# Where thirteen blocks of a cleared matrix are issued from, and when, in a graph network with expert layers on one core

## Chip, core and metric

The kernel runs on one NeuronCore of a Trainium2 chip. The metric is the device time of one execution in microseconds. TensorE (PE in the profile, its weight loads PEld), VectorE (DVE), ScalarE (ACT) and GpSimd (POOL) each have an instruction queue of their own; SyncE (SP) only issues DMAs here. DMAs issued by GpSimd are indirect ones (gathers and scatters by an index per partition).

## The reference

6250 nodes with 256 features, 100000 edges `(src, dst, edge_weight)` sorted by `dst`. The first of four layers is a graph layer, and the change lies in it. Cut to what matters:

```python
def _L0_gnn_ref(x, edge_row, edge_col, edge_vals, eps, W1, b1, g1, be1, W2, b2, g2, be2):
    msgs = edge_vals[:, None] * x[edge_col]
    agg = jax.ops.segment_sum(msgs, edge_row, num_segments=n)
    h = (1.0 + eps[0]) * x + agg
    h = _bn_relu(h @ W1 + b1, g1, be1)
    h = _bn_relu(h @ W2 + b2, g2, be2)
    return h
# called as  x = x + _L0_gnn_ref(_layernorm(x), src, dst, edge_weight, ...):
# edge_row is src, edge_col is dst
```

So every node collects, over its edges, the weighted feature rows of its neighbours. A layer of 8 experts (2 per token), a second pair of graph convolutions and a layer of 4 experts follow; the change leaves them as they are.

## The kernel before

**Two ways to sum.** The edges stand in 782 groups of 128. `dst` is sorted and dense at low numbers, so the first 395 groups (`C0`) fall on only 13 blocks (`DB`) of 128 neighbours. For those, the kernel builds a matrix `S` in DRAM: 13 blocks of 128 x 6272 cells, one cell for each pair of neighbour and node, and a spare row of cells at its end. The weights are scattered into `S`, and TensorE multiplies blocks of `S` with the neighbours' rows (`product_of_cells`). For the other groups, `scatter_items` makes 423 items, each a product and a scatter of 128 rows of 256 floats that are added into three accumulators in DRAM (`acc`, L716).

**Clearing S.** `clear_cells(b, z)` (L564) writes zeros over block `b`: one DMA of 3136 KB from a small zero tile `zz`. Block 0 and the spare tail (L834) are cleared at the start; the blocks 1 to 12 are cleared in `later_loads` (L843) after the loads of `X`. All of it is issued by SyncE. The dictionary `zeros` keeps the DMA of each block, so that scatters can wait for it.

**Comparing keys.** `cell_values(c0, c1, ...)` (L522) handles a chunk of four groups (`CB`). SyncE loads the chunk's cell keys, broadcast to all partitions (`h_kb`, L530); VectorE compares them with the keys of each edge (`h_eq`, L538, four per chunk); TensorE sums the weights of edges with the same key (`h_pa`, L544); ScalarE copies the result out (`h_sa`, L546); TensorE turns it (`h_pt`, L549); VectorE writes the values `hv` (L550, L552) and the places `hc` (L555). From group 72 (`CA`) on, a group is also compared with the group ahead of it.

**Scattering.** `scatter_cells(c)` (L572) lets GpSimd scatter the 128 values of group `c` into `S`. Groups under 72 add (`OP.add`), as groups close to each other may share cells: they are taken in four lanes of 18 groups, and each waits for the landing of the one ahead of it in its lane. The later groups only write (`OP.bypass`) and wait for nothing but the clearing of the blocks that they can reach: block `b` from group `LO[b]` on, which is 105, 152, 187, 217, 244, 267, 289, 310, 329, 347, 364 and 381 for the blocks 1 to 12.

**The order of the work.** First all chunks under group 72 are compared, then `later_loads` is called, then come the adding scatters (with seven gathers of the later items between them, L423), then the layer norm of the nodes. After that `rows_to_cells(72, 395)` (L873) goes through the other chunks: it compares up to 16 groups ahead (`AHEAD`) and scatters behind. From about group 142 on, each scatter also advances `product_of_cells` by 0.8 steps. A step loads parts of a block from `S` (`sb`, L632; on SyncE, after all scatters emitted so far), turns them (`ctp`, L641), copies them out on ScalarE (`st`, L643), multiplies (`cps`, L615) and adds to `X` on VectorE (L620). The three accumulators are cleared on the way (L184). The instructions are ordered by a scheduler, which may move an instruction ahead of others on its engine unless `tc.keep_in_program_order` pins it; waits follow from the order in which the program emits what touches the same memory.

Of the kernel before, what the change touches and what calls it, by code (L numbers as in the profile page):

```python
# [14 lines left out]
P = 128  # L15
# [28 lines left out]
DB = 13  # L44
C0 = 395
CA = 72
CB = 4
RATE0 = 0.8
RATE1 = 0.85
AHEAD = 4  # L50

SETS = [(0,), (1, 2), (3, 4, 5), (6, 7, 8), (9, 10), (11, 12)]
LANES = 4
# [2 lines left out]
SROW = NT * P  # L56
# [3 lines left out]
LO = [0] + [int(r) - 6 for r in ROW_AT[1:DB]]  # L60
# [26 lines left out]
def rows_of(t):  # L87
    return min(P, N - t * P)
# [3 lines left out]
def gnn_ffn_kernel(ctx: ExitStack, tc: tile.TileContext, a: dict, out: bass.AP):  # L92
    nc = tc.nc
# [10 lines left out]
    S = nc.dram_tensor("S", (SALL + (C0 + 1) * P,), F32, kind="Internal").ap()  # L104
# [6 lines left out]
    X = big.tile([P, NT, D], F32, name="X")  # L111
# [9 lines left out]
    def load_groups(g, src):  # L121
        t0, t1 = g * TG, (g + 1) * TG
        full = [t for t in range(t0, t1) if rows_of(t) == P]
        nc.sync.dma_start(X[:, t0:t0 + len(full), :],
                          src[t0 * P:(t0 + len(full)) * P].rearrange("(t p) d -> p t d", p=P))
        for t in range(t0 + len(full), t1):
            nc.sync.dma_start(X[:rows_of(t), t, :], src[t * P:t * P + rows_of(t)])

    def store_group(table, src, g):
        t0, t1 = g * TG, (g + 1) * TG  # L130
# [38 lines left out]
    full = const.tile([P, P], F32, name="full")  # L169
# [13 lines left out]
    def clear(k, src):  # L183
        nc.sync.dma_start(accs[k].rearrange("(p t) d -> p t d", p=P),  # L184
                          src[:, None, :].to_broadcast([P, NROW // P, D]))
# [332 lines left out]
    def across(table, r0, r1):  # L518

        return bass.AP(tensor=table.tensor, offset=table.offset + r0 * P, ap=[[0, P], [1, (r1 - r0) * P]])  # L520

    def cell_values(c0, c1, ep, ap, tp):  # L522

        n = c1 - c0
        pair = c0 >= CA
        r0 = c0 - 1 if pair else c0
        kb = ep.tile([P, CB + 1, P], F32, name="h_kb", bufs=4)
        nc.sync.dma_start(kb[:, :c1 - r0, :].rearrange("p c q -> p (c q)"), across(keys, r0, c1))  # L530
        eq = ep.tile([P, CB, 2 * P], F32, name="h_eq")
        ct = ep.tile([P, CB], F32, name="h_ct")
        wd = ep.tile([P, CB, CB], F32, name="h_wd")
        half = slice(0 if pair else P, 2 * P)
        nc.vector.tensor_tensor(wd[:, :n, :n], hw[:, c0:c1, None].to_broadcast([P, n, n]), unit[:, :n, :n], OP.mult)
        for i in range(n):
            c = c0 + i
            nc.vector.scalar_tensor_tensor(eq[:, i, half],  # L538
                                           kb[:, i:i + 1 + pair, :].rearrange("p c q -> p (c q)"),
                                           hk[:, c:c + 1], upto2[:, half], op0=OP.is_equal, op1=OP.mult,  # L540
                                           accum_out=ct[:, i:i + 1])
        pa = ap.tile([CB, 2 * P], F32, name="h_pa")
        for i in range(n):
            nc.tensor.matmul(pa[:n, half], wd[:, i, :n], eq[:, i, half], start=(i == 0), stop=(i == n - 1))  # L544
        sa = ep.tile([CB, 2 * P], F32, name="h_sa")
        nc.scalar.copy(sa[:n, half], pa[:n, half])  # L546
        pt = tp.tile([P, 2, CB], F32, name="h_pt")
        for h in range(0 if pair else 1, 2):
            nc.tensor.transpose(pt[:, h, :n], sa[:n, h * P:(h + 1) * P], ident[:n, :n])  # L549
        nc.vector.tensor_copy(hv[:, c0:c1], pt[:, 1, :n])  # L550
        if pair:
            nc.vector.tensor_tensor(hv[:, c0 - 1:c1 - 1], hv[:, c0 - 1:c1 - 1], pt[:, 0, :n], OP.add)  # L552
        nc.vector.tensor_scalar(ct[:, :n], ct[:, :n], nofit, 1.5, op0=OP.add, op1=OP.is_gt)
        nc.vector.tensor_tensor(ct[:, :n], ct[:, :n], aside[:, c0:c1], OP.mult)
        nc.vector.tensor_tensor(hc[:, c0:c1], ct[:, :n], hk[:, c0:c1], OP.add)  # L555

    zeros = {}
# [6 lines left out]
    def clear_cells(b, z):  # L564

        zw = z.shape[1]
        ins = nc.sync.dma_start(S[b * P * SROW:(b + 1) * P * SROW].rearrange("(p q w) -> p q w", p=P, w=zw),
                                z[:, None, :].to_broadcast([P, SROW // zw, zw]))
        tc.add_to_no_dep_group("cells", ins.ins)
        zeros[b] = ins.ins  # L570

# [259 lines left out]
    zz = only0.tile([P, ZW], F32, name="zz")  # L831
    nc.vector.memset(zz, 0.0)
    clear_cells(0, zz)
    rest = nc.sync.dma_start(S[SALL:].rearrange("(p q) -> p q", p=P), zz[:, :C0 + 1])  # L834
    tc.add_to_no_dep_group("cells", rest.ins)
    zeros[DB] = rest.ins
    cell_keys()
# [5 lines left out]
    def later_loads():  # L843
        nc.vector.memset(hi_i, FAR)
        g0 = EC // P
        nc.sync.dma_start(hi_i[:, :g0], ed[:g0 * P, 2 * P - 1:2 * P].rearrange("(g p) o -> p (g o)", p=P))
        nc.sync.dma_start(hi_i[:EC - g0 * P, g0:g0 + 1], ed[g0 * P:EC, 2 * P - 1:2 * P])
        for g in range(NG):
            load_groups(g, a["x"])
        nc.sync.dma_start(vec, a["vecs"])  # L850
        for b in range(1, DB):
            clear_cells(b, zz)

    with tc.tile_pool(name="cl", bufs=5) as lp, tc.tile_pool(name="clt", bufs=2, space=PSUM) as tp, \
            tc.tile_pool(name="clp", bufs=2, space=PSUM) as pp:
        product = product_of_cells(nodes, lp, tp, pp)
        next(product)
        steps = [0.0, 0]

        def advance(n, blocks=0):  # L860

            steps[0] += n
            while steps[0] >= 1:
                steps[0] -= 1
                try:
                    product.send(blocks)
                except StopIteration:
                    return

        with tc.tile_pool(name="sc", bufs=2) as ep, tc.tile_pool(name="ev", bufs=1) as gp, \  # L870
                tc.tile_pool(name="sca", bufs=2, space=PSUM) as ap, tc.tile_pool(name="sct", bufs=1, space=PSUM) as ctp:

            def rows_to_cells(c0, c1):  # L873
                cleared, valued = 0, set()
                for c in range(c0, c1, CB):
                    if c == 160:
                        item_columns(gp, ctp, evs)
                    if c >= 200 + 24 * cleared and cleared < NACC:
                        tc.keep_in_program_order(nc.vector.memset(zero, 0.0))
                        clear(cleared, zero)  # L880
                        cleared += 1
                    for e in range(c, min(c1, c + (AHEAD + 1) * CB), CB):
                        if e not in valued:
                            valued.add(e)
                            cell_values(e, min(e + CB, c1), ep, ap, ctp)
                    e = min(c + CB, c1)
                    for i in range(c - 1, e - 1 if e < C0 else e):
                        scatter_cells(i)
                        done = sum(HI[b] + 24 <= i for b in range(DB))
                        if done:  # L890
                            advance(RATE0, done)

            for j in range(0, CA // CB):
                cell_values(j * CB, (j + 1) * CB, ep, ap, ctp)
            later_loads()
            items_of_rows(ctp)
            evs = []
            for i, c in enumerate(l * LC + j for j in range(LC) for l in range(LANES)):
                if c < CA - 1:
                    scatter_cells(c)  # L900
                if i == 20:
                    evs = fetch_items(gp)
            for g in range(NG):
                mv, rstd = ln_stats(x_tiles(g))
                for i, x in enumerate(x_tiles(g)):
                    r, t = x.shape[0], g * TG + i
                    ln_apply(nodes[:r, t, :], x, mv, rstd, i)
                    nc.scalar.activation(X[:, t, :], nodes[:, t, :], AF.Copy, scale=geps)
            rows_to_cells(CA, C0)
        with tc.tile_pool(name="sg", bufs=2) as ep, tc.tile_pool(name="sw", bufs=4) as wp, \  # L910
                tc.tile_pool(name="spt", bufs=1, space=PSUM) as ptp, \
                tc.tile_pool(name="spm", bufs=2, space=PSUM) as pmp:

            def along(k):
                advance(RATE1, sum(HI[b] + 24 <= C0 + k - KF for b in range(DB)))

            scatter_items(KF, NK, nodes, (ep, wp, ptp, pmp), along)
        for _ in product:
            pass
# [42 lines left out]
    with tc.tile_pool(name="f0c", bufs=1) as fc:  # L962
# [7 lines left out]
        with tc.tile_pool(name="f0x", bufs=2) as xp, tc.tile_pool(name="f0s", bufs=1) as sp, \  # L970
# [132 lines left out]
            for e in range(X0):  # L1103
                c0 = 0
                for name, k in (("L0_ffn_ln_g", KD), ("L0_ffn_ln_b", KD), ("L0_ffn_b1", H0 // P)):
                    c = VAT[name] + e * k
# [415 lines left out]
```

## Time and profile before

| | us |
|---|---|
| median of 3 runs | 4661.52 |
| lowest, highest | 4650.03, 4668.09 |
| the profiled execution | 4696.92 |
| its span, first to last instruction | 4695.1 |
| GpSimd's first scatter into `S` (L574) | 40.26 |
| GpSimd's first scatter that only writes | 229.82 |
| last landing of the accumulators (`acc`, L716) | 1571.06 |

The table of engines at the head of the page gives busy time, share of the span and number of instructions:

```
PE 3700.9 (79%) x16130; PEld 2742.6 (58%) x16130; DVE 1950.9 (42%) x7650; ACT 1055.4 (22%) x2437; POOL 2211.6 (47%) x1914
```

The groups of instructions have one line each: line of the code, engine, operation, what is written and read, count, busy time, mean duration in ns, and the idle time of the engine just before them with what ended it. The two groups of GpSimd's queue in the first 1560 us are:

```
L716 POOL DMA_INDIRECT acc<-m,idx x423 | 657.3, 1554 | 190.0 <-issue 69.2
L574 POOL DMA_INDIRECT S<-hv,hc x395 | 429.2, 1087 | 259.4 <-issue 92.4
```

A timeline has start, duration, engine, line and operation, and in brackets the idle time ahead and its releaser. SPq is SyncE's queue of DMAs. Idle time put down to "issue" is time in which an engine waited for nothing that the profile shows.

### The profile page before, as it was taken

How to read it: one execution, taken by the hardware profiler on the slowest of the kernel's cores; microseconds unless marked ns; L12 is line 12 of the kernel's file. 1: busy time of each engine (PE TensorE's matmuls, PEld its weight loads, DVE VectorE, ACT ScalarE, POOL GpSimd, SP SyncE). 2: the span in 40 equal slices, each digit the busy share in tenths (PEclk: the TensorE clock that was granted, in tenths of full speed). 3: DMA queues.
4: the chain of work that ended last, by engine and by line, in shares of the span. 5: the costliest groups of instructions: out<-in, count | busy, mean ns of one | idle time of the engine just before them, and what ended most of it. 6: DMA issues, size and time to landing. Idle time of an engine off the chain costs nothing.

```text
span 4695.1 us, 52949 instructions
## 1 busy us (share of the span) xinstructions
PE 3700.9 (79%) x16130; PEld 2742.6 (58%) x16130; DVE 1950.9 (42%) x7650; ACT 1055.4 (22%) x2437; POOL 2211.6 (47%) x1914
## 2 busy tenths in 40 slices
PE   3407778777778576899999978888877888787999
PEld 1103446666666236788888856666646666663444
DVE  6405444334334577322121254444454444445443
ACT  2001113333333242222222230000032000005443
POOL 3676666877778200233333306666623666650000
PEclk7658889999899775999999988999998999998999
DMA  9804525666666731566667645555415554540000
GB/s 305 255 21 154 186 91 95 104 102 101 102 107 74 195 111 57 173 187 191 198 188 199 179 137 191 159 157 155 133 29 176 157 160 152 157 141 13 18 18 19
DMA packets 411033, 627.76 MB, mean 134 GB/s; under 512 B 59719, under 2 KB 317530, under 8 KB 410730
## 3 DMA queue, kind: packets, MB, share of 16 engines
q1 hardware_dynamic: 266554, 426.28, 28.1%
q0 software_dynamic: 144176, 197.85, 22.1%
q8 instruction: 140, 2.29, 0.2%
q14 instruction: 163, 1.34, 0.1%
HBM read 459.47 MB, written 165.69 MB: 133 GB/s over the span
## 4 chain that ended last, share of the span: by engine, by line
PE 53%; DVE 5%; issue 4%; DMA 3%; ACT 1%; another core or an unknown queue 0%; POOL 0%; SPq 0%; DVEq 0%; POOLq 0%; ACTq 0%
PE dps L1298 12%; PE pm L736 9%; PE ph L1199 8%; PE py L1208 8%; PE dense L270 3%; PE hid L1254 2%; PE ph L1449 2%; PE py L1474 1%; DMA g<-table,s_i 1%; PE ph L1443 1%; DVE bn_st L237 1%; PE py L1472 1%; PE pl L1006 1%; PE tp L230 1%; DMA s<-acc 1%
## 5 line engine op out<-in xcount | busy, mean ns | idle before, releaser
L731 POOL DMA_INDIRECT g<-table,s_i x846 | 804.8, 951 | 601.6 <-PE dps L1298 178.6
L716 POOL DMA_INDIRECT acc<-m,idx x423 | 657.3, 1554 | 190.0 <-issue 69.2
L1298 PE MATMUL dps<-X,wide_b 128*128 128x256 f32 (+1 forms) x2548 | 714.4, 393 | 19.3 <-issue 19.0
L736 PE MATMUL pm<-g,sw 128*128 128x256 f32 x1692 | 530.8, 404 | 224.3 <-issue 123.1
L738 DVE TENSOR_TENSOR wide<-wide,pm 128x256 f32 x846 | 354.1, 419 | 625.1 <-PE dps L1298 385.7
L1298 PEld LDWEIGHTS dps<-X,wide_b 128*128 128x128 f32 (+1 forms) x2548 | 506.0, 199 | 101.1 <-issue 26.1
L574 POOL DMA_INDIRECT S<-hv,hc x395 | 429.2, 1087 | 259.4 <-issue 92.4
L736 PEld LDWEIGHTS pm<-g,sw 128*128 128x128 f32 x1692 | 312.5, 195 | 350.9 <-issue 216.2
L602 DVE TENSOR_SCALAR sw<-lane,dl,w_e 128x128 f32<-128x128 f32 x1269 | 445.2, 364 | 115.2 <-PE dps L1298 60.4
L1199 PE MATMUL ph<-xe,we 128*128 128x256 f32 x1792 | 398.9, 381 | 0.0
L1208 PE MATMUL py<-we,hT 128*128 128x256 f32 x1792 | 396.0, 379 | 0.0
L1213 POOL DMA_INDIRECT mixed<-yo,to_i x112 | 178.1, 1590 | 450.2 <-DVE yo L1211 193.8
L615 PE MATMUL cps<-wide,st 128*128 128x256 f32 x1274 | 360.3, 410 | 19.0 <-DVE X L620 18.3
L1199 PEld LDWEIGHTS ph<-xe,we 128*128 128x128 f32 x1792 | 342.2, 191 | 47.6 <-issue 0.5
L1208 PEld LDWEIGHTS py<-we,hT 128*128 128x128 f32 x1792 | 336.2, 190 | 43.4
L752 ACT COPY hT<-tp 128x512 f32<-128x512 f32 (+1 forms) x75 | 40.6, 578 | 1362.1 <-PE tp L751 1361.9
L1201 ACT ACTIVATE hT<-ph,par 128x256 f32<-128x256 f32 x448 | 213.2, 476 | 570.8 <-PE ph L1199 565.0
L697 PE MATMUL pcs<-eq,sw 128*128 128x128 f32 x846 | 183.5, 300 | 140.8 <-DVE sw L602 96.7
L615 PEld LDWEIGHTS cps<-wide,st 128*128 128x128 f32 x1274 | 251.2, 204 | 70.1 <-DVE X L620 20.0
L712 PE MATMUL pm<-wide,cT 128*128 x846 | 268.3, 404 | 28.3 <-issue 23.8
L544 PE MATMUL h_pa<-h_eq,h_wd 128*4 128x256 f32 (+1 forms) x790 | 204.5, 398 | 108.3 <-DVE h_eq L538 103.8
L697 PEld LDWEIGHTS pcs<-eq,sw 128*128 128x128 f32 x846 | 148.1, 202 | 186.6 <-issue 97.6
(342 smaller groups left out, 4602.3 us busy)
## 6 DMA issues: line engine op xcount, KB each, us to landing
we<-in_L_ffn_W_dram SPq DMA_DIRECT2D x112, 1024.0 KB
wide_b<-S SPq DMA_DIRECT2D x182, 448.0 KB
S<-zz SPq DMA_DIRECT2D x13, 3136.0 KB
sb<-S SPq DMA_DIRECT2D x91, 448.0 KB
h_kb<-keys SPq DMA_DIRECT2D x80, 320.0 KB
acc<-zero SPq DMA_DIRECT2D x3, 6400.0 KB
s<-acc SPq DMA_DIRECT2D x72, 256.0 KB
g<-table,s_i POOLq DMA_INDIRECT x846
```

Of the source, the lines that this page charges most:

```text
L574: sc = nc.gpsimd.indirect_dma_start(out=S.rearrange("(e o) -> e o", o=1), in_=hv[:, c:c + 1], in_offset=None, compute_op=OP.add if c < CA ...
L602: nc.vector.tensor_scalar(sw, lane, dl[:, k:k + 1], w_e[:, k:k + 1], op0=OP.is_equal, op1=OP.mult)
L615: nc.tensor.matmul(ps[:, j, :], st[:, i + j, :], nodes[:, b, :], start=(y == 0), stop=(y == len(sts) - 1))
L697: nc.tensor.matmul(pc, sw, eq[:, i, :], start=True, stop=True)
L712: nc.tensor.matmul(pm, cT, nodes[:, bass.ds(bv, 1), :].rearrange("p o d -> p (o d)"), start=True, stop=True)
L716: nc.gpsimd.indirect_dma_start(out=accs[k % NACC], out_offset=bass.IndirectOffsetOnAxis(ap=idx[:, i:i + 1], axis=0), in_=m, in_offset=None ...
L731: nc.gpsimd.indirect_dma_start(out=g, out_offset=None, in_=table, in_offset=bass.IndirectOffsetOnAxis(ap=s_i[:, k:k + 1], axis=0))
L736: nc.tensor.matmul(pm[:, 0, :], sw, g, start=True, stop=True)
L738: nc.vector.tensor_tensor(at, at, pm, OP.add)
L1199: nc.tensor.matmul(ps, we1[:, k, m * P:(m + 1) * P], xe[:, k, :], start=(k == 0), stop=(k == KD - 1))
L1208: nc.tensor.matmul(ps, hT[:, m, q * P:(q + 1) * P], we2[:, m, :], start=(m == 0), stop=(m == MH - 1))
L1298: nc.tensor.matmul(ps, sb[:r, t, :], X[:r, t, :], start=(t == 0), stop=(t == NT - 1))
```

## The change

`clear_cells` issues from ScalarE's queue instead of SyncE's and is pinned in program order; so is the clear of the tail. The loop over blocks 1 to 12 goes out of `later_loads`. Instead, `clear_ahead(c)` is called ahead of the comparison of each chunk, and clears the next blocks whose first scatter `LO[b]` is at most 48 groups ahead. Block 1 so comes at group 60, blocks 2 to 12 at groups 104, 140, 172, 196, 220, 244, 264, 284, 300, 316 and 336. `load_groups` returns its DMAs; nothing uses them.

```diff
+CLEARED = 48
+
...
     def clear_cells(b, z):
 
         zw = z.shape[1]
-        ins = nc.sync.dma_start(S[b * P * SROW:(b + 1) * P * SROW].rearrange("(p q w) -> p q w", p=P, w=zw),
+        ins = nc.scalar.dma_start(S[b * P * SROW:(b + 1) * P * SROW].rearrange("(p q w) -> p q w", p=P, w=zw),
                                 z[:, None, :].to_broadcast([P, SROW // zw, zw]))
+        tc.keep_in_program_order(ins)
         tc.add_to_no_dep_group("cells", ins.ins)
         zeros[b] = ins.ins
...
     rest = nc.sync.dma_start(S[SALL:].rearrange("(p q) -> p q", p=P), zz[:, :C0 + 1])
+    tc.keep_in_program_order(rest)
     tc.add_to_no_dep_group("cells", rest.ins)
...
         nc.sync.dma_start(vec, a["vecs"])
-        for b in range(1, DB):
-            clear_cells(b, zz)
...
                     for e in range(c, min(c1, c + (AHEAD + 1) * CB), CB):
                         if e not in valued:
+                            clear_ahead(e)
                             valued.add(e)
                             cell_values(e, min(e + CB, c1), ep, ap, ctp)
...
+            def clear_ahead(c):
+
+                while len(zeros) <= DB and LO[len(zeros) - 1] <= c + CLEARED:
+                    clear_cells(len(zeros) - 1, zz)
+
             for j in range(0, CA // CB):
+                clear_ahead(j * CB)
                 cell_values(j * CB, (j + 1) * CB, ep, ap, ctp)
```

More of the change, by code (lines that the diff above doesn't have):

```diff
@@ L123, in load_groups @@
         full = [t for t in range(t0, t1) if rows_of(t) == P]
-        nc.sync.dma_start(X[:, t0:t0 + len(full), :],
-                          src[t0 * P:(t0 + len(full)) * P].rearrange("(t p) d -> p t d", p=P))
+        ins = [nc.sync.dma_start(X[:, t0:t0 + len(full), :],
+                                 src[t0 * P:(t0 + len(full)) * P].rearrange("(t p) d -> p t d", p=P))]
         for t in range(t0 + len(full), t1):
-            nc.sync.dma_start(X[:rows_of(t), t, :], src[t * P:t * P + rows_of(t)])
+            ins.append(nc.sync.dma_start(X[:rows_of(t), t, :], src[t * P:t * P + rows_of(t)]))
+        return ins
     def store_group(table, src, g):
```

## The prediction

> **What bounds the kernel now.** I read the engine table first (TensorE 79% busy, GpSimd 47%), then the chain of waits. That chain starts only at 1556.36 us, with the landing of the last `acc<-m,idx`, and everything the change touches lies before that point. So the view that decides is the busy time by stretch. These are my own cuts, with the PE, PEld, DVE, ACT and POOL busy times after the length, then clock, DMA share and GB/s:
>
> ```profile
> 64.00:120.00 56.00, 7.47 (x37) 3.50 (x36) 42.40 (x204) 24.85 (x61) 35.21 (x26) 0.53 1.08 365
> 120.00:180.00 60.00, 0.00 (x0) 0.00 (x0) 0.00 (x0) 0.00 (x0) 45.08 (x30) 0.50 1.11 349
> 184.00:230.00 46.00, 44.93 (x198) 15.11 (x198) 44.49 (x276) 6.89 (x19) 27.45 (x18) 0.94 0.59 142
> 230.00:345.00 115.00, 15.90 (x61) 6.79 (x59) 9.39 (x58) 2.52 (x6) 87.53 (x91) 0.58 0.11 27
> 345.00:702.00 357.00, 266.30 (x1132) 142.12 (x1132) 178.23 (x867) 52.73 (x131) 216.87 (x220) 0.85 0.43 140
> 702.00:1556.00 854.00, 657.91 (x3466) 546.21 (x3466) 336.19 (x1602) 315.84 (x974) 659.53 (x429) 0.91 0.66 98
> ```
>
> GpSimd is the only engine that works in all six, and each of its DMA issues is followed by 0.30 us of issue gap. In 702:1556 that makes 659.5 + 429 x 0.30 = 788 of 854 us; in 230:345 it makes 87.5 + 91 x 0.30 = 115 of 115. So up to 1556 us **GpSimd's queue is the clock**, and an early saving there reaches the end only if the queue does not lose it again at 345 to 702, where it idles. The timeline of SyncE's queue shows what the diff moves:
>
> ```profile
> 64.28 100.69 SPq L567 DMA_DIRECT2D S<-zz  x12
> 165.08 67.05 SPq L530 DMA_DIRECT2D h_kb<-keys  x25
> 322.14 0.32 SPq L632 DMA_DIRECT2D sb<-S  x1
> ```
>
> The twelve clears hold SyncE's queue for 100.69 us and the rings at 350 to 365 GB/s. The comparisons' loads (L530) come behind them, so VectorE stands still for 77 us. But that stall is not the price: GpSimd has 72 adding scatters to issue meanwhile, is done with them at 229.8, and then finds 92 later groups waiting (no gap over 0.30 us until 345). What the clears cost is in GpSimd's own rows (start, duration, gap ahead):
>
> ```profile
> 81.36 1.54 POOL L574 DMA_INDIRECT S<-hv,hc  x1 [0.30 <-DMA S<-hv,hc]
> 83.22 1.54 POOL L574 DMA_INDIRECT S<-hv,hc  x1 [0.32 <-DMA S<-hv,hc]
> 87.27 1.54 POOL L574 DMA_INDIRECT S<-hv,hc  x1 [2.51 <-DMA S<-hv,hc]
> 89.20 1.54 POOL L574 DMA_INDIRECT S<-hv,hc  x1 [0.39 <-DMA S<-hv,hc]
> ...
> 209.23 1.54 POOL L574 DMA_INDIRECT S<-hv,hc  x1 [0.82 <-DMA S<-hv,hc]
> 214.15 1.54 POOL L574 DMA_INDIRECT S<-hv,hc  x1 [3.38 <-DVE h_eq L538]
> 218.27 1.67 POOL L574 DMA_INDIRECT S<-hv,hc  x1 [2.58 <-DMA S<-hv,hc]
> ```
>
> An add waits for an earlier one of its lane, a distance d back in the queue (the built program lists the waits). A gap ends when that one has landed, so start minus start is its latency L. At d = 3, 89.20 - 81.36 = 7.84 us beside the clears; 5.1 to 6.9 before 64 us beside the loads of X; 4.1 to 5.4 at the end, after the clears (d = 1: 218.27 - 214.15 = 4.12).
>
> **The change, part by part.**
>
> *Adding scatters.* Each add costs the larger of 1.84 us (1.54 + 0.30) and L/d. Before, of 72 adds, 6 stand at d = 1, 12 at 2, 15 at 3, 32 at 4, 7 are free; and 7 fetches (L423) take 1.3 us each. With L = 5.4 to 6.3 early, 7.85 in the clears and 4.6 at the end: d1 2 x 5.4 + 4 x 4.6 = 29.2; d2 4 x 3.15 + 5 x 3.9 + 3 x 2.3 = 39.0; d3 11 x 2.62 + 4 x 1.84 = 36.2; d4 32 x 1.96 = 62.7; free 7 x 1.84 = 12.9; fetches 9.1; sum 189.1. Measured from 40.26 to the first plain scatter at 229.82: 189.6. So the form holds. After, the built order has 4, 11, 15, 35 and 7. Only block 1 is cleared in this stretch (at group 60, near 60 us; its ACT wait is one old DMA); block 2, due at group 104, waits for all scatters up to group 86. So L is 7.85 for some 10 us, else 5.4 to 6.3 early and 4.6 later: d1 2 x 5.4 + 2 x 4.6 = 20.0; d2 6 x 3.15 + 5 x 2.3 = 30.4; d3 3 x 2.62 + 12 x 1.84 = 29.9; d4 35 x 1.84 = 64.4; free 12.9; fetches 9.1; sum 166.7. **Gain 189.6 - 166.7 = 23 us**; its floor is 0 (L unchanged), its ceiling 48 (all at 1.84).
>
> Two rules of the Trainium skill speak against this. "DMA: Bandwidth & Descriptors", section "Issuing engines are not separate DMA queues", says a second issuing engine saves only the issue time, as all transfers share 16 engines. By it alone, 0: SyncE's issue time bounds nothing. I agree about *who*, but the clears also move in *time*, and the row prices that: 7.84 against 4.12. "SBUF — State Buffer", section "SBUF: two separate sides", says GpSimd cannot write descriptors while VectorE holds their shared port; its example loses 2.5 us per DMA. The moved comparisons now run beside the adds, so by the rule L = 7.1 and about 12 adds at d = 3 cost 0.5 us more: gain 17. The trace differs: in 120:180 VectorE is at 0.00 and L is 7.7 to 8.9, in 184:230 it is busy 44.49 of 46 us and L falls to 4.1. I keep 23.
>
> *Start-up.* Moving block 0's clear and pinning the tail clear (L834) reorders the start. In the built program, block 0's clear waits on ScalarE behind the sortedness flag (L371), two groups of X are issued on SyncE before the branch instead of one, and the join after the branch now waits for block 0's clear with both groups beside it. That is 2 x 0.92 - 0.2 MB (the tail clear leaves) = 1.6 MB at 0.38 MB/us (what the rings moved at 12 to 18 us) = 4.3 us later than 21.6. Statistics of group 0 (L211, 0.40 us each) now stand ahead of the first key, about 1.2 us. **Cost +5.5 us**; between 0 (if the X loads drain first) and 8.
>
> *SyncE's queue.* 100.69 us leave it. Worth nothing by itself: VectorE works earlier, for scatters which GpSimd cannot issue earlier. `sb<-S` (L632) still waits for scatters near group 142, as before.
>
> *The clears on ScalarE.* Eleven (blocks 2 to 12) now wait on ScalarE for all scatters emitted before them, 18 groups behind the comparison that follows. Queued behind are `h_sa` (L546) and `st` (L643), for which TensorE, then VectorE, then GpSimd wait. Cover: at such a clear GpSimd still has 17 valued groups, 17 x 1.27 = 21 us, and the first new chunk needs about 5. Where GpSimd itself starves (345:702, gaps of 74.6 us beyond 0.30), group e-18 is long done. So the wait is 0; without the cover it would be one scatter's latency, 4.6. The issue takes 0.6 to 1.1 us (SyncE's unblocked rows for the same transfer).
>
> *Contention at 345:702.* Nine or so clears of 3.2 MB (9 us each) fall there. Ceiling: a scatter's landing 7.85 instead of 4.6 (+3.25), an `sb` load at half rate (+2.5), the issue (+0.85): 6.6 us each. Floor 0: three clears of `acc` (L184), 6.55 MB each at 422, 460 and 510 us in the same stretch, leave GpSimd's gaps at 24 us in 420 to 540 against 25 in 560 to 680. That row is nearest; I take 0.5 us for each of eleven, **+5 us**.
>
> **Sum:** -23 + 5.5 + 5 = -12. The profiled execution took 4696.92 (span 4695.1), so 4684.9; the median of the runs is 35.4 below the profiled one, so **4650 us**.
>
> **Rivals.** (A, 0.42) as summed; own range 4636 to 4668. (B, 0.26) *Start-up costs nothing and the comparisons' lead removes GpSimd's 10.4 us stall at 345*: -23 - 10 + 0 = -33, 4628. For it: X's loads end earlier. Against: that stall follows the first `sb`, which waits as before. (C, 0.09) *An add's latency stays* because comparisons' loads and VectorE now run beside it: +5.5 + 5, 4672. Against: 184:230 has both. (D, 0.23) *The coupled stretch pays*: each clear falls on the loop scatter, `sb`, TensorE, comparison, scatter, which already has the 74.6 us of gaps, and adds up to 6.6: -17 + 11 x 6.6 = +56, 4717. It decides from 1.6 us a clear, and makes the kernel slower by 0.5% from (17 + 23)/11 = 3.7. Against it stand the `acc` clears; for it, that those ran in SyncE's own queue order, not across it. That the change does not do what it says is part of C and D: "48 ahead" is 18 at most once the clear waits for scatters.
>
> **Numbers.** 0.5% is 23 us, about what this kernel's measurement can tell from no change. Faster: B and a little of A, 0.30; same: most of A and C, 0.47; slower: D, 0.23. The range 4618 to 4697 takes in B with more gain and the lower part of D.
>
> **What would show it.** First scatter at 45 to 46 us instead of 40.26; the first plain scatter near 212 instead of 229.8; GpSimd's wait for `S<-hv,hc` well under 53.7 us; gaps at the coupled stretch near 80 us; the first `acc` scatter (L716) some 12 us earlier. Gaps over 115 us there mean D; a d = 3 spacing still near 7.8 us means C.

## The result, and the profile after

The changed kernel takes 4682.75 us (median, 4675.60 to 4697.86) against 4662.35 us (4645.78 to 4680.95) for the kernel before in the same comparison: a ratio of **1.0049, 95% interval 1.0035 to 1.0062**. It is slower by some 20 us where I forecast 12 us faster. The profiled execution took 4687.44 us (span 4685.7). Lines of the changed file stand 3 or 4 further down there: the scatter is L578, the clear L570, `h_kb` L533, `sb` L636.

The busy time by stretch, with the cuts of the prediction (PE, PEld, DVE, ACT, POOL, clock, DMA share, GB/s):

```profile
64.00:120.00 56.00, 19.18 (x84) 5.85 (x84) 49.70 (x261) 24.09 (x64) 39.48 (x27) 0.63 0.56 137
120.00:180.00 60.00, 17.52 (x78) 6.41 (x76) 21.50 (x133) 2.17 (x6) 49.94 (x34) 0.65 0.43 72
230.00:345.00 115.00, 51.21 (x182) 18.99 (x182) 36.32 (x203) 7.36 (x19) 78.72 (x80) 0.66 0.36 111
345.00:702.00 357.00, 252.19 (x1055) 135.67 (x1056) 168.89 (x810) 48.66 (x124) 200.85 (x206) 0.82 0.65 218
702.00:1556.00 854.00, 673.64 (x3519) 557.21 (x3517) 341.86 (x1632) 316.74 (x976) 659.52 (x435) 0.91 0.65 97
```

The first two rows are what the change was meant to give: the rings are half idle (0.56 and 0.43 where they stood at 1.1), and GpSimd issues 61 instructions instead of 56. The loss is in the next two: 80 instead of 91 instructions at 230 to 345 us, 206 instead of 220 at 345 to 702 us, with the DMA share up from 0.43 to 0.65. The timelines of SyncE's and ScalarE's DMA queues show where the clears went:

```profile
70.37 229.56 SPq L533 DMA_DIRECT2D h_kb<-keys  x25
...
70.89 0.52 ACTq L570 DMA_DIRECT2D S<-zz  x1
230.77 0.52 ACTq L570 DMA_DIRECT2D S<-zz  x1
292.20 0.52 ACTq L570 DMA_DIRECT2D S<-zz  x1
...
311.35 0.32 SPq L636 DMA_DIRECT2D sb<-S  x1
```

Ten of the twelve stand between 292 and 633 us, beside the product of cells. GpSimd's own rows (start, duration, gap ahead), and its waits up to 760 us (total, times, longest), first of the kernel before and then of the changed one:

```profile
203.29 1.54 POOL L578 DMA_INDIRECT S<-hv,hc  x1 [0.30 <-issue]
205.14 1.54 POOL L578 DMA_INDIRECT S<-hv,hc  x1 [0.30 <-issue]
208.85 1.54 POOL L578 DMA_INDIRECT S<-hv,hc  x1 [2.17 <-DMA S<-hv,hc]
210.70 0.99 POOL L578 DMA_INDIRECT S<-hv,hc  x1 [0.30 <-issue]
```

```profile
POOL S L574 <- DMA S<-hv,hc: 53.7, 46, 4.5
POOL S L574 <- DVE hv L552: 51.8, 21, 4.4
POOL S L574 <- DVE h_wd L535: 30.6, 8, 10.4
```

```profile
POOL S L578 <- DVE hv L555: 95.9, 21, 10.3
POOL S L578 <- DMA S<-hv,hc: 24.6, 15, 5.1
...
POOL S L578 <- DVE h_wd L538: 4.0, 2, 3.7
```

The adds' wait for each other fell from 53.7 to 24.6 us, and the first scatter that only writes starts at 210.70 instead of 229.82 us. The wait for values from VectorE (`hv`) rose from 51.8 to 95.9 us; part of this is a change of name, as the wait put down to `h_wd` of the same comparisons fell, and the two together rose from 82.4 to 99.9 us. The last scatter into `S` starts at 734.42 instead of 718.90, the first into `acc` at 748.28 instead of 737.66: a lead of 19 us has become a lag of 11 to 16.

### The profile page after: what moved, and what is told of

It reads as the page before. It is cut to its first block, busy times and chain, and to the rows that moved or that the text cites. A ratio compares the mean times of both kernels' runs of the same rounds, so it can differ in the third digit from the quotient of the medians.

```text
span 4685.7 us, 53016 instructions
## 1 busy us (share of the span) xinstructions
PE 3723.0 (79%) x16130; PEld 2763.1 (59%) x16130; DVE 1957.5 (42%) x7650; ACT 1051.9 (22%) x2436; POOL 2208.8 (47%) x1914
## 3 DMA queue, kind: packets, MB, share of 16 engines
q1 hardware_dynamic: 243050, 384.53, 25.5%
## 4 chain that ended last, share of the span: by engine, by line
PE 65%; issue 10%; DVE 8%; DMA 7%; another core or an unknown queue 4%; POOL 3%; ACT 2%; DVEq 0%; SPq 0%; POOLq 0%; ACTq 0%
PE dps L1308 12%; PE pm L740 9%; PE ph L1209 8%; PE py L1218 8%; DMA acc<-m,idx 4%; PE cps L619 4%; PE dense L273 3%; PE h_pa L547 2%; PE hid L1264 2%; PE ph L1459 2%; PE pm L716 2%; POOL S L578 2%; PE pcs L701 1%; PE py L1484 1%
## 5 line engine op out<-in xcount | busy, mean ns | idle before, releaser
L1308 PEld LDWEIGHTS dps<-X,wide_b 128*128 128x128 f32 (+1 forms) x2548 | 510.1, 200 | 99.4 <-issue 22.9
L578 POOL DMA_INDIRECT S<-hv,hc x395 | 429.3, 1087 | 268.5 <-issue 103.3
L547 PE MATMUL h_pa<-h_eq,h_wd 128*4 128x256 f32 (+1 forms) x790 | 215.4, 416 | 33.5 <-DVE h_eq L541 27.9
```

The lines of the kernel that those rows point to most:

```text
L578: sc = nc.gpsimd.indirect_dma_start(out=S.rearrange("(e o) -> e o", o=1), in_=hv[:, c:c + 1], in_offset=None, compute_op=OP.add if c < CA ...
L1308: nc.tensor.matmul(ps, sb[:r, t, :], X[:r, t, :], start=(t == 0), stop=(t == NT - 1))
```

## The experiments

Chips differ by more than the change does. On some, the kernel before takes 4660 to 4690 us (the chip of the comparison is one), on others 4420. Each chip was used at one time only, so the chip and the moment are not told apart. Times are therefore compared by their ratio to before on the same chip. "Gaps" in the table is GpSimd's idle time beyond 0.30 us an instruction, from the first scatter that only writes to the last, added up from the timeline of one profile; the three starts are from the same timeline. At 4660 to 4690 us the only profile of the kernel before is the one of the prediction, so starts and gaps there are compared across chips.

| kernel | ratio to before, 95% | first scatter | first that only writes | last one | gaps |
|---|---|---|---|---|---|
| *before at 4420 us* | | | | | |
| before (e8) | | 41.02 | 232.43 | 646.18 | 2.9 |
| changed (e5) | 1.0027, 1.0014 to 1.0039 | 44.91 | 210.22 | 656.43 | 33.9 |
| changed (e15) | 1.0019, 1.0006 to 1.0033 | 45.51 | 209.29 | 653.73 | 33.3 |
| no wait (e1) | 1.0036, 1.0025 to 1.0048 | 48.32 | 219.32 | 666.82 | 38.2 |
| SyncE issues (e2) | 1.0036, 1.0024 to 1.0048 | 49.77 | 210.06 | 662.45 | 37.5 |
| start-up of before (e3) | 1.0015, 1.0005 to 1.0025 | 41.53 | 209.24 | 653.13 | 31.6 |
| the same (e14) | 1.0007, 0.9997 to 1.0017 | 40.50 | 206.66 | 651.62 | 32.1 |
| no wait, start-up of before (e16) | 1.0027, 1.0016 to 1.0038 | 40.68 | 212.80 | 655.10 | 30.4 |
| before, ScalarE issues (e4) | 0.9998, 0.9986 to 1.0011 | 40.44 | 230.42 | 644.18 | 3.1 |
| clears of `acc` earlier (e7) | 0.9993, 0.9984 to 1.0003 | 40.67 | 207.85 | 641.62 | 19.9 |
| wait only (e13) | 0.9953, 0.9937 to 0.9969 | 41.52 | 206.86 | 625.70 | 6.4 |
| **spread (e6)** | **0.9941, 0.9925 to 0.9958** | 40.87 | 206.68 | 623.34 | 5.3 |
| *before at 4660 to 4690 us* | | | | | |
| before (its profile) | | 40.26 | 229.82 | 718.90 | 77.3 |
| changed (its profile) | 1.0049, 1.0035 to 1.0062 | 46.63 | 210.70 | 734.42 | 111.7 |
| changed (e18) | 1.0012, 0.9992 to 1.0031 | 44.41 | 209.42 | 747.03 | 127.9 |
| eight chunks ahead (e9) | 1.0047, 1.0029 to 1.0064 | 39.02 | 203.99 | 747.91 | 132.7 |
| clears of `acc` later (e10) | 1.0061, 1.0039 to 1.0084 | 40.93 | 207.35 | 748.06 | 127.2 |
| no wait, start-up of before (e12) | 1.0023, 1.0009 to 1.0037 | 41.33 | 214.71 | 727.35 | 102.3 |
| **spread (e11)** | **0.9984, 0.9972 to 0.9996** | 41.43 | 205.20 | 723.20 | 106.0 |
| wait only (e17) | 0.9993, 0.9976 to 1.0011 | 40.82 | 204.45 | 722.29 | 106.4 |

(e11 and e12 are on one chip, e17 and e18 on another, e9 and e10 on a third; e5 to e8 on one, e1 to e4 on one, e13 to e16 on one.)

**Wait or traffic, issuer, start-up.** My theory after the result: the stretch in which scatters, loads of `sb`, TensorE and comparisons run in a loop pays for the clears, by ScalarE's wait for scatters (W) or by their traffic (T).

```diff
 # e1: the clear waits for no scatter; each block is cleared ahead of its first scatter
         tc.keep_in_program_order(ins)
+        tc.declare_no_dep(ins.ins, group="cells", keep=[], reason="...")
 # e2: nc.scalar.dma_start -> nc.sync.dma_start in clear_cells
 # e3: block 0 by nc.sync, not pinned; the tail not pinned
 # e4: e3, and all of blocks 1 to 12 in later_loads, by nc.scalar
```

> The changed kernel, in which each clear on ScalarE no longer waits for the scatters emitted before it (none of them has a place in the block that it clears); places in the queues stay. Theory W (the wait on ScalarE holds comparisons and transposed copies back): GpSimd's gaps beyond 0.30 us at 212 to 720 us fall from 97 to about 75 us, the last plain scatter starts near 705 instead of 734, and the time is 15 to 30 us below the changed kernel's 4682.75. Theory T (the clears' traffic slows scatters and the loads of sb): the clears still fall in the same stretch, so gaps stay at 90 to 100 us and the time within 8 us of the changed kernel.

> The changed kernel with the clears at the same places, in SyncE's queue. Theory W: ScalarE's queue is free, so its comparisons go on; SyncE has loads of sb that wait for scatters anyway, so most of the loss goes: 10 to 25 us below 4682.75. If what is behind the waiting clear matters whichever queue it is in (loads of keys are there instead), it stays within 8 us or gets slower. Theory T: as the changed kernel, within 8 us.

> The changed kernel with the start-up of before: the clears of block 0 and of the tail on SyncE, not pinned; blocks 1 to 12 as in the changed kernel. First scatter back at 40 us instead of 46.6. If a later start is carried to the end, 5 to 6 us below 4682.75; if GpSimd's waits further on swallow it, within 2 us.

> The kernel before with one difference: clears of blocks 1 to 12 stand together ahead of the first plain group, as before, but are issued by ScalarE. If the issuer costs nothing, the time of before (4662) within 8 us: ScalarE's queue is then full for about 100 us in place of SyncE's, and adds see the same 7.8 us latency. If ScalarE as issuer is itself dear, 4675 or more.

All four had before at 4421 us, which my expectations in microseconds had not foreseen; the differences can still be read. Without the wait (e1), gaps stay at 38.2, and with SyncE as issuer (e2), whose clears still wait for scatters, at 37.5: at 4420 us W falls. Moving the issuer alone (e4) is worth nothing, 0.9998. With the start-up of before, the first scatter is back at 41.53.

**What the clears meet.** In those profiles the gaps are few and large: 15 us near 450 and 9 us near 515 us, with VectorE waiting for `h_kb`. Before them, SyncE's queue stands behind a clear of `acc` (6400 KB). So one kernel spreads the block clears over the time in which GpSimd issues without a gap, and one moves the clears of `acc` instead. The two kernels themselves run beside them.

```diff
 # e6: e3, and in clear_ahead
-                while len(zeros) <= DB and LO[len(zeros) - 1] <= c + CLEARED:
+                while len(zeros) <= DB and 88 + 8 * (len(zeros) - 2) <= c:
 # e7: e3, and in rows_to_cells
-                    if c >= 200 + 24 * cleared and cleared < NACC:
+                    if c >= 112 + 24 * cleared and cleared < NACC:
```

> The changed kernel itself, beside the others on one chip, for the milestones. Ratio to before 1.0035 to 1.0062 as measured; if the start-up accounts for 10 us more than the scatters' start shows (the kernel with the start-up of before measured 1.0015), the first scatter is 6 us late and the rest of the difference lies behind the last scatter. Gaps of GpSimd between the first and the last plain scatter near 32 us, as with the start-up of before.

> Start-up of before; the twelve clears of blocks 1 to 12 on ScalarE, one per 8 groups ahead of the comparisons of groups 88 to 176, so that they run while GpSimd issues plain scatters without a gap (about 210 to 330 us) and none meets the clears of acc. Theory T (the clears' cost is their meeting with the clears of acc in a stretch where loads of keys are due): first plain scatter near 209, gaps behind it near 3 us, last plain scatter near 623, time 18 to 24 us below before, ratio 0.9945 to 0.996. If a clear costs 2 to 3 us wherever it lies behind the adds: gaps near 30 us and ratio 1.000 to 1.002.

> Start-up of before, the clears of blocks 1 to 12 as in the changed kernel, but the three clears of acc 88 groups earlier (at groups 112, 136 and 160 in place of 200, 224 and 248), where three of the block clears stand at most. Theory T: the 15 us and 9 us gaps go, gaps fall from 32 to under 10 us, last plain scatter near 630, ratio to before 0.995 to 0.998. If block clears slow the coupled stretch by themselves: gaps stay at 25 us or more, ratio near 1.0015.

> The kernel before, one profile on the chip of the other runs: first scatter 40.3, first plain scatter near 230, last plain scatter near 644 and gaps near 3 us, as in the kernel whose clears ScalarE issues together.

SyncE's queue at the second clear of `acc`, in the kernel before (e8):

```profile
431.15 0.54 SPq L184 DMA_DIRECT2D acc<-zero  x1
431.74 17.35 SPq L530 DMA_DIRECT2D h_kb<-keys  x1
```

The load of keys behind it is held for 17.35 us, and GpSimd's longest gap after it is 1.6 us: the chunks already compared just cover it. The changed kernel (e5), in order of time, from the timelines of SyncE, ScalarE, GpSimd and VectorE:

```profile
415.66 0.54 SPq L187 DMA_DIRECT2D acc<-zero  x1
416.25 24.74 SPq L533 DMA_DIRECT2D h_kb<-keys  x1
423.19 0.52 ACTq L570 DMA_DIRECT2D S<-zz  x1
435.76 0.96 POOL L578 DMA_INDIRECT S<-hv,hc  x1 [0.31 <-issue]
448.88 0.48 DVE L541 SCALAR_TENSOR_TENSOR h_eq<-h_kb,hk,upto 128x256 f32<-128x256 f32 x1 [15.98 <-DMA h_kb<-keys]
451.80 0.96 POOL L578 DMA_INDIRECT S<-hv,hc  x1 [15.08 <-DVE hv L555]
```

A block clear starts 7.5 us into the clear of `acc`, the hold grows to 24.74 us, and GpSimd runs out of values at 436. The longer hold is 7.4 of the 13.5 us by which the gap is longer than in e8. Some 4 us more are a shorter cover: when the clear of `acc` starts, e5 has values ready for 5 groups more than it has scattered, e8 for 8, at 1.27 us each. A meeting just before had taken from it: the clear of `acc` at 379.42 and a block clear at 386.20, with a gap of 4.57 us at 416. A third gap, 10.48 us at 518, follows the meeting at 464.97 and 467.38 by 50 us. The load that it waits for also stands behind a block clear at 501.40, so that it belongs to the meeting is likely, not shown. Beyond the 0.30 us of every issue the three gaps make 29 of the 33.9 us. In the spread kernel (e6) no block clear is near, and the hold is that of before:

```profile
409.73 0.64 SPq L187 DMA_DIRECT2D acc<-zero  x1
410.42 17.47 SPq L533 DMA_DIRECT2D h_kb<-keys  x1
```

Its gaps are 5.3 us, and the lead of the adds (206.68 against 232.43) arrives at the last scatter (623.34 against 646.18) and in the time, 0.9941. In e7 two pairs are left, and one gap. Rows of SyncE, ScalarE, VectorE and GpSimd:

```profile
275.67 0.52 ACTq L570 DMA_DIRECT2D S<-zz  x1
278.75 0.75 SPq L187 DMA_DIRECT2D acc<-zero  x1
314.72 0.48 DVE L541 SCALAR_TENSOR_TENSOR h_eq<-h_kb,hk,upto 128x256 f32<-128x256 f32 x1 [24.06 <-DMA h_kb<-keys]
...
349.67 0.52 SPq L187 DMA_DIRECT2D acc<-zero  x1
361.03 0.52 ACTq L570 DMA_DIRECT2D S<-zz  x1
385.57 0.96 POOL L579 DMA_INDIRECT S<-hv,hc  x1 [17.80 <-DVE h_ct L556]
```

At the first pair VectorE waits 24.06 us for keys, but at 290 us values are ready for 29 groups, 37 us of GpSimd's work at 1.27 us each, and GpSimd has no gap. At the second the cover is short, and the gap is 17.80 us. Behind it seven block clears start between 399.66 and 550.71 us with no clear of `acc` beside them, and GpSimd has no gap over 1 us. So on this chip a block clear costs next to nothing alone, and next to a clear of `acc` it costs what the hold exceeds the cover. The forecast for e7, gaps under 10 us and 0.995 to 0.998, missed: the second pair costs its 18 us gap, and the ratio is 0.9993.

**A longer cover, and no meeting, on a chip of the other kind.** Both of these had before at 4665 us.

```diff
 # e9: e3, AHEAD = 8 and CLEARED = 32 in place of 4 and 48
 # e10: e3, and  c >= 320 + 24 * cleared  for the clears of acc
```

> Start-up of before, block clears and acc clears in place (each as many groups ahead of the scatters as in the changed kernel), but comparisons run up to eight chunks (32 groups) ahead of the scatters instead of four (16), so that ScalarE, VectorE and SyncE have twice the cover of GpSimd's queue. If a pair of clears costs only what its hold of SyncE's loads exceeds the cover: the holds of 23 to 25 us stay, the gaps fall from 32 to under 10 us, ratio 0.995 to 0.998. If scatters themselves are slowed by the pair, gaps stay over 25 us and the ratio near 1.0015.

> Start-up of before, block clears as in the changed kernel, the three clears of acc behind the last block clear (groups 320, 344, 368 in place of 200, 224, 248). If only pairs cost: no gap over 6 us between 340 and 560 us although eight block clears stand there. Their own cost at the end: the three come closer together, and loads of sb are behind them, so a gap of up to 20 us may open after 560 us; ratio 0.995 to 1.001.

Both missed. In e9 the gaps are 132.7 us and the ratio is 1.0047, but the run does not test the cover, for the cover did not get longer: when its three clears of `acc` start, values are ready for 6, 5 and 1 groups more than GpSimd has scattered, against 7, 7 and 1 in the changed kernel. In e10, with the clears of `acc` out of the way there were still gaps of 3 to 8 us all through 340 to 560 us, and a new one of 22.9 us at 697 where the late clears stand, and the ratio is 1.0061. What holds at 4420 us is not the whole at 4660 us. So the spread kernel and the one without waits were tried again, and came upon such a chip (before at 4686 us):

> The kernel of e6_spread once more, for a chip of the kind on which the kernel before takes 4660 us and its GpSimd has 77 us of gaps behind the first plain scatter (against 4420 us and 3 us elsewhere). If the clears cost only where they meet the coupled stretch, gaps there fall from the changed kernel's 112 to about 77 us, the last plain scatter starts near 698 instead of 734 and the ratio to before is 0.993 to 0.997. If on such a chip a clear costs 3 us anywhere behind the adds, gaps are 100 us or more and the ratio 1.000 or more. On a chip of the other kind: 0.994 as before.

> Start-up of before; clears of blocks 1 to 12 on ScalarE at the places of the changed kernel, without their wait for scatters. On a chip of the 4660 us kind: if ScalarE's wait is what makes the gaps there, they fall from 112 to under 90 us and the ratio to 0.996 to 1.000; if it is the clears' traffic, they stay over 105 us and the ratio over 1.003. On the other kind: gaps near 32 us, ratio near 1.0015, as with the wait.

Spread, the change is faster than before here as well, 0.9984, and below the kernel that keeps the traffic in place without the wait (1.0023, whose adds are 9.5 us slower, since two clears now start at 127.65 and 149.12 beside them). But the spread kernel's gaps are 106.0 us, not 77: the gaps are as forecast for a clear that costs 3 us anywhere, the ratio is not. The gaps of e12, 102.3 us, fall between its two forecasts (under 90, over 105).

Where the gaps stand says more than their sum. The same gaps, split at the scatters of groups 160 and 216 (about 335 and 435 us):

| kernel | groups 72 to 160 | 160 to 216 | 216 to the last |
|---|---|---|---|
| before (its profile) | 0.5 | 26.7 | 50.1 |
| changed (its profile) | 11.3 | 28.3 | 72.1 |
| changed (e18) | 14.4 | 24.2 | 89.4 |
| eight chunks ahead (e9) | 14.1 | 30.2 | 88.4 |
| clears of `acc` later (e10) | 8.5 | 31.4 | 87.3 |
| no wait (e12) | 0.4 | 28.9 | 73.0 |
| spread (e11) | 21.4 | 31.7 | 52.9 |
| wait only (e17, below) | 16.4 | 32.4 | 57.7 |

Behind group 216, kernels with whole clears there have 72 to 89 us, those without 50 to 58. Ahead of group 160, the six with ScalarE's wait have 8 to 21 us, and the two without it under 1. The rows show how the wait acts, first ScalarE's in the kernel before, then ScalarE's and GpSimd's in the changed kernel, then GpSimd's first gap in e12:

```profile
234.87 0.36 ACT L546 COPY h_sa<-h_pa 4x256 f32<-4x256 f32 x1 [1.84 <-issue]
327.90 0.36 ACT L546 COPY h_sa<-h_pa 4x256 f32<-4x256 f32 x1 [92.67 <-issue]
```

```profile
230.77 0.52 ACTq L570 DMA_DIRECT2D S<-zz  x1
231.39 0.63 ACT L549 COPY h_sa<-h_pa 4x256 f32<-4x256 f32 x2 [95.79 <-DMA S<-hv,hc]
...
285.04 0.36 ACT L549 COPY h_sa<-h_pa 4x256 f32<-4x256 f32 x1 [25.53 <-remote]
288.27 0.96 POOL L578 DMA_INDIRECT S<-hv,hc  x1 [7.78 <-DVE hv L555]
```

```profile
340.19 0.96 POOL L580 DMA_INDIRECT S<-hv,hc  x1 [4.26 <-DVE hv L555]
```

Before, the comparisons run on to group 160 by 240 us, when GpSimd stands at group 80. In the changed kernel the clear of block 2 holds ScalarE's copies for 95.79 us, values are ready for 16 groups at 230 us, and a wait of 25.53 us uses these up. It is put down to `remote`, with no releaser shown. In e12 values stand ready up to group 164 by 180 us. Since e12 also has no clear between 149 and 339 us, the wait is not parted from the traffic by a run; but from 259 to 285 us, where ScalarE waits, no clear runs: the one at 230.77 takes some 9 us, and the next starts at 292.20.

**Wait without traffic.** Most of each block is cleared early, and only a fourteenth at the changed kernel's place with its wait.

```diff
 # e13, e17: e3, and in clear_ahead
+                while len(most) + 1 < DB and 88 + 8 * len(most) <= c:
+                    clear_cells(len(most) + 1, zz, 1, 14, most)
                 while len(zeros) <= DB and LO[len(zeros) - 1] <= c + CLEARED:
-                    clear_cells(len(zeros) - 1, zz)
+                    clear_cells(len(zeros) - 1, zz, 0, 1)
```

> Start-up of before. Thirteen fourteenths of each block of 1 to 12 are cleared while GpSimd issues plain scatters without a gap (one block per 8 groups, as in e6_spread); the last fourteenth (0.23 MB) stands where the changed kernel's clear stands, on ScalarE and with its wait for scatters. The coupled stretch keeps the waits and loses the traffic. If traffic is the price: as the spread clears, ratio near 0.994 on a 4420 us chip and near 0.998 on a 4660 us chip. If the wait is: near the changed kernel with the start-up of before, 1.0015 and about 1.0035.

> The kernel of e3_start again (changed kernel, start-up of before), beside the others of this call. If the start-up is 4 to 6 us of the difference on either kind of chip, 0.001 below e15_changed; if it is swallowed, equal to it.

> The changed kernel, on the chip of this call: 1.0027 on a 4420 us chip, 1.0049 on a 4660 us chip.

> The kernel of e12_no_wait_start again: traffic without the wait. If traffic is the price, within 0.001 of e14_start; if the wait is, 0.002 or more below it.

> The kernel of e13_wait_only (0.9953 on a 4420 us chip) for a chip of the 4660 us kind. If traffic is the price there too: near the spread clears' 0.9984, at most 1.000. If ScalarE's wait is the price on such a chip: 1.003 or more.

> The changed kernel beside it: 1.0035 to 1.0062 on a chip of the 4660 us kind, 1.002 to 1.003 on the other.

Before took 4421.57 us beside e13 to e16. GpSimd's waits for `hv` from 240 to 640 us, first with the wait alone (e13), then with wait and traffic (e14), then with the traffic alone (e16):

```profile
POOL S L582 <- DVE hv L555: 3.8, 4, 2.3
```

```profile
POOL S L579 <- DVE hv L555: 27.1, 4, 14.9
```

```profile
POOL S L580 <- DVE hv L555: 26.1, 5, 15.8
```

At 4420 us traffic is the price, the wait is not: e13 keeps the waits and has 0.9953, e14 has 1.0007. Taking the wait away (e16) was expected to leave the time within 0.001, and does worse: 1.0027 against 1.0007, with the first plain scatter 6 us later, as two clears then run beside the adds. The start-up is 1.0019 less 1.0007, 5 us, though the two intervals overlap. At 4688 us (e17, e18), the wait alone gives 0.9993 and the changed kernel 1.0012; the intervals overlap, so the times of this pair do not settle it there. The 1.0012 also lies under the 1.0035 to 1.0062 that I had expected: the size of the loss differs from chip to chip.

## Why the prediction was wrong

- **Adding scatters, -23:** right. From the first scatter to the first one that only writes, 189.56 us became 164.07, where the sum had 189.1 and 166.7: -25.5. At 4420 us it is -24 to -28 (e3, e5, e6, e7, e13, e14 and e15 against e8). The cause is what the rings carry beside the adds: with all clears left beside them but issued by ScalarE (e4) the stretch keeps 189.98 us, and with two more of them there (e16) it is 6 us longer than without these (e14). The rule of the Trainium skill that I set aside ("SBUF — State Buffer", "SBUF: two separate sides") asked for a gain of 17 in my sum. That left out the adds at d = 1 and 2; with L = 7.1 for these too it would be about 6, an estimate in the same form. The trace gave 25.5, with VectorE busy for 21.50 us of 120 to 180 where it had stood still; whether its comparisons hold the shared port at all, no run shows.
- **Start-up, +5.5:** right. 6.4 us at the first scatter, 3.9 (e5 against e8) and 5.0 us (e15 against e14) elsewhere; about 5 us in the time, with intervals that overlap.
- **Who issues, 0:** right. e4 has 0.9998, as the Trainium skill has it ("DMA: Bandwidth & Descriptors", "Issuing engines are not separate DMA queues"). e2, at 1.0036, is no faster than the changed kernel on two other chips at 4420 us (1.0019 and 1.0027).
- **Contention at 345:702, +5, "I take 0.5 us for each of eleven": this failed.** Where before takes 4420 us, the changed kernel's gaps grew from 2.9 to 33.3 and 33.9 us, 2.8 us a clear. In the profiles of the comparison they grew by 22 us behind group 216, where the whole clears stand. The row that I took the size from was the gaps beside three clears of `acc` alone. It was read rightly: alone they cost nothing. But it showed a hold of 17 us under a cover that was not yet used up, and I carried it over as if a second transfer would be free too. The two add up in one hold (17.35 to 24.74 us), and what exceeds the cover is gap. At 4420 us three gaps carry 29 of the 34 us, two of them behind a pair beyond doubt; the other clears are nearly free, so an average over eleven was the wrong form. In the comparison only the clears at 504.93 and 509.02 us start within 10 us of each other, with a gap of 9.29 us; why the others cost there too stays open.
- **The clears' wait on ScalarE, 0, "GpSimd still has 17 valued groups": right at 4420 us (e13), not on the chip of the comparison.** The 17 groups came as said (16 at 230 us), but before had 80 at 240 us, and the `remote` waits on this chip outlast 16. The gaps ahead of group 160 grew by 11 us. That these are the wait's is likely from the rows, not shown by a run of its own.
- **The gain carried through 345:702:** I named the condition ("only if the queue does not lose it again") and then put nothing for it. At 4420 us nearly all of it is kept (e6: 25.8 us ahead at the first plain scatter, 22.8 at the last, 26 in the time). On the slower chips it is lost: e11 and e17 clear no whole block behind 390 us, are 25 us ahead of before's profile at the first plain scatter, and 3 to 4 us behind it at the last; their times gain 0.16% and 0.07%, the second within its error. Of their 25 us, 16 to 21 go ahead of group 160.

In the comparison's profiles the sum is then -25.5 + 6.4 + 34.6 (from 489.1 to 523.7 us between the first and the last plain scatter), +15.5 at the last plain scatter, and 20 us between the medians. Of the 34 us of gaps 11 stand ahead of group 160, 2 from there to group 216, and 22 behind that. **Rival D** named the place and the sign ("the coupled stretch pays", slower by 0.5% from 3.7 us a clear), but not the mechanism: it reckoned with 6.6 us from a slower scatter, load and issue at every clear. **C** is out, since the wait for adds fell to 24.6 us. **B** is out where it was tried: with the start-up of before the kernel is still not faster (1.0015, 1.0007). Of the signs announced, the first scatter (46.63), the first plain scatter (210.70 for 212) and the adds' wait came as said. The gaps did not (94 us at 345 to 702, for 80), and neither did the first scatter into `acc`, 10.6 us later in place of 12 us earlier.

**Open:** what fills the coupled stretch on the slower chips. The profile there has many waits put down to `remote`. The kernel before, 345 to 702 us (total, times, longest):

```profile
ACT h_sa L546 <- PE h_pa L544: 114.5, 32, 23.0
ACT h_sa L546 <- remote: 102.6, 15, 19.4
...
DVE X L620 <- remote: 38.9, 5, 17.2
```

`h_sa` and `X` take results of TensorE. TensorE itself halts there inside a run of matmuls that wait for nothing in the trace, as here in e10:

```profile
593.43 0.38 PE L620 MATMUL cps<-wide,st 128*128 128x256 f32 x1 [0.37 <-issue]
595.53 0.38 PE L620 MATMUL cps<-wide,st 128*128 128x256 f32 x1 [1.73 <-issue]
596.26 0.46 PE L620 MATMUL cps<-wide,st 128*128 128x256 f32 x1 [0.35 <-issue]
```

From 212 to 745 us the `remote` waits add up, over all engines, to 237 us before, 323 and 384 us in the changed kernel, and none in any profile at 4420 us. They are 242 us in e12, which has the clears' traffic but not the wait, and 322 us in e11, which spreads the traffic: they do not simply grow with the traffic. That TensorE's halts are the bound of that stretch fits; no run took them away, so it is not shown.

## What to carry to other kernels

A row that shows a transfer doing no harm may show only that its hold (the time for which it keeps later loads waiting) is still under the cover (the work that the waiting engines have done ahead). Before adding a second transfer beside it, compare the longer hold with the cover, in microseconds, and ask what the last hold left of that cover. A large clear belongs where the engine that sets the pace has work queued and waits for no DMA: here that is the run of plain scatters at 206 to 350 us. Moved there with the old start-up, the same clears beat the kernel before on both kinds of chip (0.9941 where before takes 4420 us, 0.9984 at 4686). Which engine issues a clear decided nothing here. What stands behind a waiting clear in the same queue can matter: it cost nothing that could be measured at 4420 us, but on the slower chips it cut a lead of 80 groups to 16, and gaps followed that neither kernel without the wait has.

## What the runs showed of the hardware

- The same kernel took 4420 us on some chips and 4660 to 4690 us on others, with clocks of 0.904 to 0.913 against 0.891 to 0.896 in the profiled executions. GpSimd's gaps in one and the same stretch were 2.9 and 77.3 us: a stretch that has slack on one chip has none on another, and the spread kernel's ratio of 0.994 becomes 0.998.
- A DMA issue on SyncE's queue stood for 17.35 us behind a clear of 6400 KB, and for 24.74 us when a clear of 3136 KB from ScalarE's queue joined it: 7.4 us more for a transfer that takes some 9 us by itself, 3136 KB at the 350 to 365 GB/s of the kernel before. Two queues did not keep the two clears apart.
